# Macaron block on one core: uneven halves of the products with v, pieces behind the smaller half, row additions on GpSimd, VectorE's side work regrouped

## The chip, the core and the metric

One core of a Trainium2 chip runs the whole program. The metric is the device time of one execution in microseconds. TensorE (PE) multiplies, VectorE (DVE) and ScalarE (ACT) read the products from PSUM, GpSimd (POOL) works on SBUF alone, SyncE (SP) issues most DMAs. All data is float32.

## The reference, cut to what matters

```python
x = x + 0.5 * ffn(layernorm(x), ...)      # 8 experts, capacity 1.25 N / E; an expert chosen too often is dropped whole
x = x + attn(layernorm(x), ...)           # 16 heads of 16, causal softmax over 1024 tokens, 8 sequences
x = x + 0.5 * ffn(layernorm(x), ...)
# in ffn: probs = softmax(x @ gate_w.T); top 2 experts; keep = counts <= cap
```

x has 8 x 1024 tokens of 256 numbers. With these inputs every expert is chosen more often than its capacity allows, so both feed-forward parts add nothing; the kernel counts the choices of both gates in any case, and computes the experts only in a branch that this run does not enter. What is timed is the attention with its two gates.

## The kernel before, in words

The work goes by sequence b (8) and by group g of four heads (4): a **unit** u = 4 b + g, 32 in all. For each unit `project` makes q and k in transposed form (`pq`, one bank for each half of the tokens), packs them (`packed`) and sends them by DMA into `qTs` and `kTs` (four buffers each). Two passes over the scores follow.

- `m_steps` (line 852) multiplies q with k (`sm`), and VectorE takes the row maxima: `tensor_reduce` into `first` for a block wholly below the diagonal, a masked add-and-maximum (the row CUSTOM_DVE, with its DVE_READ_ACCUMULATOR into `top`) for a block that ends on it. `settle` transposes the maxima and sends them into a row of `qTs`.
- `e_steps` (line 898) multiplies k with q again (`sc`); the row of maxima is subtracted by the product itself. ScalarE takes the exponential into `pT`, GpSimd masks the diagonal block (the row TENSOR_SCALAR_AFFINE_SELECT), and `values` (line 927) multiplies by v, with a column of ones that gives the softmax's sums, into `pav`.

The two passes are interlaced by hand: at each of 24 **steps** k of a unit TensorE gets the `sc` tiles of unit u and the `sm` tiles of unit u + 1 in turn (line 1240), two of each, for one block and two heads. The widths of the blocks by step are 512, 512, 384, 384, 256, 256, 128, 128 for k = 0 to 7, then 512 eight times (k = 8 to 15, plain maxima), then again 512 down to 128 in pairs (k = 16 to 23, masked). Each step's tiles take four of six PSUM banks in rotation (`score`, line 700), so the third and fourth tile of a step take the banks of the first and second tile of the step before.

`values` of a block runs in two parts, at steps k + 2 and k + 3 (lines 1247 and 1248): the columns in two halves (line 937), or all in the first part when the block is 256 wide or less. So for the wide blocks part 0 falls on odd steps and part 1 on even ones.

Everything else goes **beside** the steps. A generator in `Beside` asks either for a number of steps to pass, or for a place: `PIECE` and `QK` wait until `step(kinds)` offers one, and `REST` asks for the next step, so that a matrix product of two halves is spread over two steps. After each step's products, `beside.step` is called once (lines 1278 to 1283): `QK` first at k = 0 and 8, `PIECE` at the steps in `long_steps` (0 to 3 and 8 to 19). Pieces are the four transposes of `turned`, the eight v products of `values_of` (`pv`) and the eight output products of `leave` (`px`) for each sequence. What a generator issues between its yields goes to the engines in the same place in their order:

- `prepare(b)` (732) loads x and takes its mean and variance on VectorE (`ln_stats`: BATCH_NORM_STATS2 and AGGREGATE) one tile of 128 rows every second step, from g = 3 on; `enter(b)` normalizes on GpSimd (`xn_a`) and transposes.
- `values_of` (774) copies v to `vaug` on ScalarE and the gate's logits on VectorE (799). `residual(b)` (805) adds the bias to x on GpSimd.
- `leave(b, hf)` (974) divides by the sums, multiplies with Wo into `px`, adds the row to x on VectorE (1017), and appends the statistics of the new row to `light`, one of which is taken at each step (1252). Then it stores the rows.
- `gate_first(b)` (815) and `regate(b)` (1103) choose two experts for each row (`choose`, 339: some twenty small VectorE operations named mx, lc, cand, first, oh, sm, prob, key, best, with an exponential on ScalarE; _f for the first gate and _g for the second) and add to a tally. `gate_first` starts at g = 0, k = 9; `regate` follows `leave(b - 1, 1)` and runs late in g = 1.

On every engine the order of issue is kept (`InOrder`, line 27), so an instruction that waits holds all behind it on its engine. Unit 31 has no scores of a next unit beside it and a loop of its own (line 1214), and `leave_last` finishes the last four heads.

Of the kernel before, what the change touches and what calls it, by code (L numbers as in the profile page):

```python
# [52 lines left out]
class Beside:  # L53
# [25 lines left out]

    def step(self, kinds=()):  # L80
        self.now += 1
        self.due()
        if self.open is not None:
            self.advance(self.open)
            return
        for kind in kinds:
            for work in self.works:
                if work[1] == kind:
                    self.advance(work)
                    return  # L90
# [12 lines left out]
def macaron_kernel(  # L103
# [112 lines left out]
    def weights(pool, bank, matmul, transpose):  # L216
# [15 lines left out]
        with nc.allow_non_contiguous_dma(reason="two vectors of 256"):  # L232
            nc.sync.dma_start(out=boT, in_=bo.rearrange("(c p) -> p c", p=P))
            nc.sync.dma_start(out=bvT, in_=bkv[D:].rearrange("(c p) -> p c", p=P))
        gpsimd.tensor_scalar(bkqT[64:], bkqT[64:], QSCALE, None, ALU.mult)

        def turn(wsb, dst, scale=None):
# [101 lines left out]
    def choose(rp, tag, n, lg):  # L339
        def new(name, shape=(P, n, E), dt=F32):  # L340
            return rp.tile(list(shape), dt, tag=f"{name}{n}", name=f"{name}_{tag}")

        def over_e(a):
            return a.unsqueeze(2).to_broadcast([P, n, E])

        mx = new("mx", (P, n))
        vector.tensor_reduce(mx, lg, AX.X, ALU.max)
        lc = new("lc")
        vector.tensor_tensor(lc, lg, over_e(mx), ALU.subtract)
        prob = new("prob")  # L350
        yield 1
        scalar.activation(prob, lc, AF.Exp)
        yield 1
        cand = new("cand")
        ohs = [new(f"oh{k}") for k in range(2)]

        def lowest(oh):
            vector.tensor_tensor(cand, cand, iota_e.unsqueeze(1).to_broadcast([P, n, E]), ALU.add)
            first = new("first", (P, n))
            vector.tensor_reduce(first, cand, AX.X, ALU.min)  # L360
            vector.tensor_tensor(oh, cand, over_e(first), ALU.is_equal)


        vector.tensor_scalar(cand, lc, 0.0, -100.0, ALU.is_equal, ALU.mult)
        lowest(ohs[0])
        yield 1
        sm = new("sm", (P, n))
        vector.tensor_reduce(sm, prob, AX.X, ALU.add)
        vector.reciprocal(sm, sm)
        vector.tensor_tensor(prob, prob, over_e(sm), ALU.mult)  # L370
        yield 1

        key = new("key")
        vector.tensor_scalar(key, prob, TINY, 1.0, ALU.is_ge, ALU.subtract)
        vector.scalar_tensor_tensor(key, key, 1e30, lc, ALU.mult, ALU.min)
        vector.scalar_tensor_tensor(key, ohs[0], -1e32, key, ALU.mult, ALU.add)
        yield 1
        best = new("best", (P, n))
        vector.tensor_reduce(best, key, AX.X, ALU.max)
        vector.tensor_tensor(cand, key, over_e(best), ALU.is_equal)  # L380
        yield 1
        vector.tensor_scalar(cand, cand, -100.0, None, ALU.mult)
        lowest(ohs[1])
        yield 1
        return prob, ohs
# [300 lines left out]
    def attention(run_no, src, dst, gate0, logits, tally):  # L686
# [3 lines left out]
        with stack:  # L690
# [40 lines left out]

            def prepare(b):
                xb = xbs[b] = ap.tile([P, TB, D + E], F32, tag="xa", name=f"xa{b}", bufs=3)
                nc.sync.dma_start(out=xb[:, :, :D], in_=src[b].rearrange("(j p) d -> p j d", p=P))
                yield 2
                st, mv = ln_tiles(f"a{b}")
                for j in range(TB):
                    ln_stats(xb, j, st, mv)
                    yield 2
                stds[b] = norm.tile([P, TB], F32, tag="std", name=f"std{b}")  # L740
                lns[b] = mv, ln_rstd(mv, f"a{b}", stds[b])
                yield 2
# [31 lines left out]
            def values_of(b, apart, j0=0, j1=TB):  # L774
# [7 lines left out]
                for j in range(j0, j1):  # L782
# [15 lines left out]
                    )  # L798
                    vector.tensor_copy(lg[:, j, :], pv[:, D : D + E])
                    if apart and j + 1 < TB:  # L800
# [22 lines left out]
            def project(u, parts=(0, 512)):  # L823
                b, g = divmod(u, NG)
                xnT = xnTs[b]
                for s0 in parts:
# [17 lines left out]
                    for k in range(8):  # L844
                        r = 32 * (k % 4)
                        nc.sync.dma_start(  # L846
                            out=(kTs, qTs)[k // 4][u % 4][r : r + HD, s0 : s0 + 512],
                            in_=packed[HD * k : HD * (k + 1), :],
                        )
# [48 lines left out]
            def e_steps(u):  # L898
# [28 lines left out]
                def values(hf, jb, pTs, part):  # L927
# [4 lines left out]
                    if w <= 256:  # L932
                        cols = slice(0, w)
                        if part == 1:
                            return
                    else:
                        cols = slice(part * w // 2, (part + 1) * w // 2)
                    for pr in (1, 0):
# [24 lines left out]
                for hf in range(2):  # L963
                    for jb in range(4 * hf + 4):
                        pTs = {}
                        yield (lambda h, hf=hf, jb=jb, pTs=pTs: scores(hf, jb, 1, pTs, h)), None
                        yield (
                            (lambda h, hf=hf, jb=jb, pTs=pTs: scores(hf, jb, 0, pTs, h)),
                            (lambda part, hf=hf, jb=jb, pTs=pTs: values(hf, jb, pTs, part)),
                        )  # L970

            def leave(b, hf):
# [28 lines left out]
                for i in range(TB // 2):  # L1003
# [3 lines left out]
                    for c in range(DC):  # L1007
# [7 lines left out]
                        if c + 1 < DC:  # L1015
                            yield REST
                    vector.tensor_tensor(xb[:, j, :], px[:, : D + E], xb[:, j, :], ALU.add)
                    light.append(lambda j=j: ln_stats(xb, j, *gate_lns[b]))
                rows = slice(hf * 512, hf * 512 + 512)
# [83 lines left out]
            def regate(b, j0, j1):  # L1103
# [4 lines left out]
                rstd = ln_rstd(gate_lns[b][1][:, j0:j1, :], f"g{b}_{j0}")  # L1108
                yield 3
                lg = logits[:, b * TB + j0 : b * TB + j1, :]  # L1110
# [32 lines left out]
            vaugs = [fixed.tile([P, TB, NH * VW + 32 - VW], F32, name=f"vaug{run_no}_{k}") for k in range(2)]  # L1143
            for qT in qTs:
                gpsimd.memset(qT, 0.0)
            for vaug in vaugs:
                gpsimd.memset(vaug[:, :, : NH * VW].rearrange("p t (h r) -> p t h r", r=VW)[:, :, :, HD:], 1.0)
                gpsimd.memset(vaug[:, :, NH * VW :], 1.0)
            for kT in kTs[:2]:
# [8 lines left out]
            for j0 in (0, HT):  # L1158
                for j in range(j0, j0 + HT):
                    ln_stats(xb, j, st, mv)  # L1160
                part = slice(j0, j0 + HT)
                rstds.append(ln_rstd(mv[:, part, :], f"a0_{j0}", stds[0][:, part]))
            for hf in range(2):
                xns = []
# [10 lines left out]
            opening = beside.add(chain(some(turning, 2), project(1), values_of(0, 0, 0, HT)))  # L1175
            owed, light, last, ons = deque(), deque(), [], {}
            STEPS = 24

            long_steps = [*range(4), *range(8, 20)]
            for u in range(-1, NU):  # L1180
                b, g = divmod(u, NG)
                if u == 0:
                    beside.finish(opening)
                    preparing = beside.add(prepare(1))
                    opening = beside.add(values_of(0, 0, HT, TB), first=True)
                    projecting = beside.add(project(2))
                    beside.add(chain((PIECE,), turning, residual(0), gate_first(0)))
                if u >= 0 and g == 2 and b + 1 < B:
                    beside.finish(entering)
                    valuing = beside.add(values_of(b + 1, 0, 0, HT))  # L1190
                if u >= 0 and g == 3 and b + 1 < B:
                    beside.finish(valuing)
                    valuing = beside.add(chain(values_of(b + 1, 0, HT, TB), residual(b + 1)))
                if u > 0:
# [3 lines left out]
                if g == 3 and u >= 0:  # L1198
                    if b + 2 < B:
                        preparing = beside.add(prepare(b + 2))  # L1200
                if u > 0 and g == 0:
# [12 lines left out]
                for k in range(0, STEPS, 2) if u == NU - 1 else ():  # L1214
# [10 lines left out]
                    if k == 0:  # L1225
                        beside.add(divided(b, 1, 8, 12, ons[1][:, 1], (1, 3, 3, 3)))
                    if k == 0:
                        beside.add(settle(u, 1), first=True)
# [8 lines left out]
                for k in range(STEPS) if 0 <= u < NU - 1 else ():  # L1237
# [11 lines left out]
                    while owed and owed[0][0] <= now:  # L1249
                        _, then, part = owed.popleft()  # L1250
                        then(part)
                    if light:
                        light.popleft()()
# [4 lines left out]
                    if g == 3 and k == 9:  # L1258

                        beside.add(leave(b, 0))  # L1260
                    if g == 0 and b and k == 9:

                        beside.add(gate_first(b))
                    if g == 0 and b and k == 2:
                        beside.add(chain(leave(b - 1, 1), regate(b - 1, 0, TB)))
                    if g == 1 and k == 7 and b + 1 < B:
# [11 lines left out]
                    if u == 0:  # L1278
                        beside.step((PIECE, QK))
                    elif k in (0, 8):  # L1280
                        beside.step((QK, PIECE))
# [9 lines left out]
            for k, _ in enumerate(leave_last(B - 1, 1, last.pop(), (scalar.copy, vector.tensor_copy))):  # L1291
                for _ in range(3 if k < 2 else len(beside.works) * STEPS):
                    beside.step()
# [65 lines left out]
```

## Time and profile before

| what | before |
| --- | --- |
| median of 3 runs | 1375.16 us (1372.16 to 1376.97) |
| the profiled execution | 1375.38 us |
| its span, first to last instruction | 1373.6 us |
| granted TensorE clock, mean | 0.987 |
| start of the first and of the last of the 744 interlaced steps | 53.6 us, 1318.9 us |
| length of a unit with g = 0, 1, 2, 3 (units 12 to 15) | 41.2, 42.4, 39.8, 39.9 us |
| copy of v to vaug, 128x256, ScalarE | 373 ns x 64 |
| addition of a row, xa<-px,xa, 128x264, VectorE | 427 ns x 64 |
| copy of logits, 128x8, VectorE | 159 ns x 64 |
| statistics of a tile, VectorE | 421 and 182 ns x 64 for each of st_g, mv_g |
| addition of the bias, 128x528, GpSimd | 1308 ns x 32 |

A row of a group has the line, the engine, the operation, the tiles written and read, the shapes and the count, then busy time and mean duration, then the idle time before it and what ended it. All operations of the attention are recorded at line 37, since they pass through `InOrder`, so groups are told apart by tiles. In a timeline the columns are start, duration, engine, line, operation, tiles, shapes, count, and in brackets the idle time before. One float32 matmul of the program shows as two instructions.

### The profile page before, as it was taken

How to read it: one execution, taken by the hardware profiler on the slowest of the kernel's cores; microseconds unless marked ns; L12 is line 12 of the kernel's file. 1: busy time of each engine (PE TensorE's matmuls, PEld its weight loads, DVE VectorE, ACT ScalarE, POOL GpSimd, SP SyncE). 2: the span in 40 equal slices, each digit the busy share in tenths (PEclk: the TensorE clock that was granted, in tenths of full speed). 3: DMA queues.
4: the chain of work that ended last, by engine and by line, in shares of the span. 5: the costliest groups of instructions: out<-in, count | busy, mean ns of one | idle time of the engine just before them, and what ended most of it. 6: DMA issues, size and time to landing. Idle time of an engine off the chain costs nothing.

```text
span 1373.6 us, 51244 instructions
## 1 busy us (share of the span) xinstructions
PE 1336.6 (97%) x20664; PEld 445.5 (32%) x20664; DVE 1038.2 (76%) x3417; ACT 785.5 (57%) x1790; POOL 398.1 (29%) x720
## 2 busy tenths in 40 slices
PE   6999999999999999999999999999999999999994
PEld 2333333333333333333333333333333333333331
DVE  3877677887787877877788777788777787787854
ACT  3256665565655565556665656656665556555562
POOL 3034114341235213152141411424123521312321
PEclk9899999999999999999999999999999999999997
DMA  4011111121121211212021211212112111121101
GB/s 142 18 27 42 42 43 56 55 72 42 53 65 49 83 31 48 74 52 77 21 58 60 84 46 37 60 57 73 42 54 58 53 49 34 50 74 42 60 27 34
DMA packets 67024, 73.73 MB, mean 54 GB/s; under 512 B 24688, under 2 KB 42232, under 8 KB 66776
## 3 DMA queue, kind: packets, MB, share of 16 engines
q1 hardware_dynamic: 65688, 69.82, 17.4%
q8 instruction: 165, 2.70, 0.8%
q14 instruction: 83, 0.68, 0.2%
q10 hardware_dynamic: 1088, 0.53, 0.1%
HBM read 26.87 MB, written 26.20 MB: 39 GB/s over the span
## 4 chain that ended last, share of the span: by engine, by line
PE 95%; DVE 3%; DMA 1%; issue 1%; POOL 0%; ACT 0%; SPq 0%; ACTq 0%; POOLq 0%
PE sc L37 42%; PE pav L37 24%; PE sm L37 10%; PE pq L37 9%; PE pv L37 5%; PE px L37 4%; PE pta L37 1%; DVE sm L37 1%; DMA bkqT<-in_L_attn_bq_dram 0%; DVE cand_g L37 0%; SPq L846 0%; PE px_last L37 0%; DVE top L37 0%; DVE first_g L37 0%; DVE oh_g L37 0%
## 5 line engine op out<-in xcount | busy, mean ns | idle before, releaser
L37 ACT ACTIVATE pT<-sc 128x512 f32<-128x512 f32 (+3 forms) x1536 | 668.9, 488 | 518.1 <-PE sm L37 381.4
L37 PE MATMUL sm<-kT,qT 32*64 32x512 f32 (+3 forms) x6144 | 752.8, 510 | 4.2 <-DVE top L37 2.2
L37 PE MATMUL sc<-qT,kT 32*64 32x512 f32 (+3 forms) x6144 | 693.8, 507 | 0.0
L37 DVE TENSOR_REDUCE first<-sm 128x1 f32<-128x512 f32 x512 | 328.7, 685 | 123.3 <-PE sm L37 122.6
L37 POOL TENSOR_SCALAR_AFFINE_SELECT pT<-pT 128x256 f32<-128x256 f32 x512 | 207.6, 408 | 735.4 <-ACT pT L37 734.9
L37 PE MATMUL pav<-pT,vaug 128*32 128x256 f32 (+2 forms) x5120 | 381.8, 370 | 2.2 <-POOL pT L37 1.5
L37 DVE CUSTOM_DVE_ANT_0 sm<-sm,causal 128x256 f32<-128x256 f32 (+3 forms) x512 | 241.8, 514 | 90.8 <-PE sm L37 80.3
L37 DVE CUSTOM_DVE_ANT_0 sm<-sm,causal,first 128x256 f32<-128x256 f32 (+3 forms) x512 | 261.4, 556 | 54.3 <-PE sm L37 48.5
L37 PEld LDWEIGHTS sc<-qT,kT 32*64 32x64 f32 x6144 | 183.1, 130 | 345.9 <-ACT pT L37 266.8
L37 PEld LDWEIGHTS sm<-kT,qT 32*64 32x64 f32 x6144 | 210.8, 130 | 33.4 <-DVE top L37 21.5
L37 PEld LDWEIGHTS pav<-pT,vaug 128*32 128x32 f32 x5120 | 102.5, 108 | 362.3 <-issue 282.7
L37 DVE DVE_READ_ACCUMULATOR2_ANT top<- 128x1 f32 x1024 | 145.5, 142 | 0.0
L37 PE MATMUL pq<-xnT,wkqT 128*32 128x512 f32 x1024 | 136.5, 608 | 1.3 <-ACT xnT L37 1.3
L37 PE MATMUL pv<-wvT,xnT 128*32 128x264 f32 x1024 | 81.1, 391 | 0.0
L37 PE MATMUL px<-woT,on 128*32 128x264 f32 x960 | 76.3, 390 | 0.0
L37 POOL TENSOR_SCALAR xn_a<-xa,mv_a,rstd_a 128x256 f32<-128x256 f32 x56 | 67.5, 1221 | 0.0
L37 ACT ACTIVATE packed<-pq,bkqT 128x512 f32<-128x512 f32 x64 | 45.4, 710 | 11.7 <-PE pq L37 11.7
L37 POOL TENSOR_TENSOR xa<-xa,bo_all 128x528 f32<-128x528 f32 x32 | 41.8, 1308 | 14.3 <-issue 13.7
L37 POOL TENSOR_TENSOR on<-on,inv 128x512 f32<-128x512 f32 (+1 forms) x32 | 40.3, 1282 | 14.1 <-DMA inv<-inv_d 14.1
L37 PEld LDWEIGHTS pq<-xnT,wkqT 128*32 128x32 f32 x1024 | 25.9, 110 | 55.5 <-issue 52.0
L37 PEld LDWEIGHTS pv<-wvT,xnT 128*32 128x32 f32 x1024 | 29.6, 110 | 41.8 <-ACT att L37 18.9
L37 PEld LDWEIGHTS px<-woT,on 128*32 128x32 f32 x960 | 27.3, 109 | 37.3 <-ACT att L37 11.4
(122 smaller groups left out, 430.8 us busy)
## 6 DMA issues: line engine op xcount, KB each, us to landing
att_d<-att SPq DMA_DIRECT2D x62, 256.0 KB
kT<-packed SPq DMA_DIRECT2D x256, 32.0 KB
qT<-packed SPq DMA_DIRECT2D x256, 32.0 KB
out_dram<-xa SPq DMA_DIRECT2D x16, 512.0 KB
on<-att_d SPq DMA_DIRECT2D x30, 256.0 KB
inv<-inv_d SPq DMA_DIRECT2D x30, 256.0 KB
xa<-in_L_attn_x_dram SPq DMA_DIRECT2D x7, 1024.0 KB
xa<-in_L_attn_x_dram SPq DMA_DIRECT2D x2, 512.0 KB
```

The costliest lines, as they stand in the source:

```text
L37: i = call(*args, **kwargs)
```

## The change

1. `values` cuts a block of 512 columns at 160 instead of 256; part 0 has 160 columns, part 1 has 352. Blocks of 384 are still halved.
2. For g other than 1 (and not in the last two units), pieces are begun only at k = 2, 10, 13 and 17, and the second half of a piece is not taken at k = 14 and 18, so it lands at 3, 11, 15 and 19. For g = 1 the places stay as they were.
3. In `leave`, ScalarE copies the product's row to SBUF (`row`), and GpSimd adds it to x, in steps k = 8 to 16 or at the end of `leave`. The rows of `leave_first` and `leave_last` are still added by VectorE.
4. Statistics in `light` are taken only at k = 8 to 15 of g = 1 and 2. `prepare` waits 32 steps after its load and then takes one tile at each step, which puts it at k = 8 to 15 of g = 0. `regate` starts at g = 2, k = 9, `gate_first` at g = 3, k = 8 (for the last sequence at the start of unit 31), `residual` at g = 0, k = 9. `choose` and `regate` yield less.
5. The logits are copied by ScalarE.
6. At the start, the scaling of bkqT and most memsets come behind the first statistics on GpSimd, and four of the eight DMAs of each packed half of unit 0 go to ScalarE's queue. In the tail one pause is shorter.

```diff
-    def step(self, kinds=()):
+    def step(self, kinds=(), rest=True):
...
         if self.open is not None:
-            self.advance(self.open)
+            if rest:
+                self.advance(self.open)
             return
...
-        gpsimd.tensor_scalar(bkqT[64:], bkqT[64:], QSCALE, None, ALU.mult)
...
         scalar.activation(prob, lc, AF.Exp)
-        yield 1
...
-            def prepare(b):
+            def prepare(b, wait, apart):
...
-                yield 2
+                yield wait
...
-                    yield 2
+                    yield apart
...
-                    vector.tensor_copy(lg[:, j, :], pv[:, D : D + E])
+                    scalar.copy(lg[:, j, :], pv[:, D : D + E])
...
-                        nc.sync.dma_start(
+                        (nc.scalar if u == 0 and k < 4 else nc.sync).dma_start(
...
-                        cols = slice(part * w // 2, (part + 1) * w // 2)
+                        cut = 160 if w == 512 else w // 2
+                        cols = slice(cut, w) if part else slice(0, cut)
...
+            def add_row():
+                xb, j, row, stats = adds.popleft()
+                gpsimd.tensor_tensor(xb[:, j, :], row, xb[:, j, :], ALU.add)
+                light.append(lambda: ln_stats(xb, j, *stats))
...
-                    vector.tensor_tensor(xb[:, j, :], px[:, : D + E], xb[:, j, :], ALU.add)
-                    light.append(lambda j=j: ln_stats(xb, j, *gate_lns[b]))
+                    row = ap.tile([P, D + E], F32, tag="row", name=f"row{b}_{j}", bufs=4)
+                    scalar.copy(row, px[:, : D + E])
+                    adds.append((xb, j, row, gate_lns[b]))
+                yield 2
+                while adds:
+                    add_row()
...
-                yield 3
+                yield 1
...
-            for qT in qTs:
-                gpsimd.memset(qT, 0.0)
-            for vaug in vaugs:
-                gpsimd.memset(vaug[:, :, : NH * VW].rearrange("p t (h r) -> p t h r", r=VW)[:, :, :, HD:], 1.0)
-                gpsimd.memset(vaug[:, :, NH * VW :], 1.0)
+            gpsimd.memset(qTs[0], 0.0)
...
-                    preparing = beside.add(prepare(1))
+                    preparing = beside.add(prepare(1, 2, 2))
...
-                    beside.add(chain((PIECE,), turning, residual(0), gate_first(0)))
+                    beside.add(chain((PIECE,), turning, residual(0)))
...
-                    valuing = beside.add(chain(values_of(b + 1, 0, HT, TB), residual(b + 1)))
+                    valuing = beside.add(values_of(b + 1, 0, HT, TB))
...
-                        preparing = beside.add(prepare(b + 2))
+                        preparing = beside.add(prepare(b + 2, STEPS + 8, 1))
...
-                    if light:
+                    if adds and 8 <= k <= 16:
+                        add_row()
+                    if light and 8 <= k < 16 and g in (1, 2):
                         light.popleft()()
...
-                    if g == 0 and b and k == 9:
-
+                    if g == 3 and k == 8:
                         beside.add(gate_first(b))
                     if g == 0 and b and k == 2:
-                        beside.add(chain(leave(b - 1, 1), regate(b - 1, 0, TB)))
+                        beside.add(leave(b - 1, 1))
+                    if g == 0 and b and k == 9:
+                        beside.add(residual(b))
+                    if g == 2 and b and k == 9:
+                        beside.add(regate(b - 1, 0, TB))
...
+                    elif g != 1 and u < NU - 2 and k not in (0, 8):
+
+                        beside.step((PIECE,) if k in (2, 10, 13, 17) else (), k not in (14, 18))
...
-                for _ in range(3 if k < 2 else len(beside.works) * STEPS):
+                for _ in range((1, 3)[k] if k < 2 else len(beside.works) * STEPS):
```

More of the change, by code (lines that the diff above doesn't have):

```diff
@@ L1162, in attention @@
                 rstds.append(ln_rstd(mv[:, part, :], f"a0_{j0}", stds[0][:, part]))
+            if gate0 is not None:
+                gpsimd.tensor_scalar(bkqT[64:], bkqT[64:], QSCALE, None, ALU.mult)
+            for qT in qTs[1:]:
+                gpsimd.memset(qT, 0.0)
+            for vaug in vaugs:
+                gpsimd.memset(vaug[:, :, : NH * VW].rearrange("p t (h r) -> p t h r", r=VW)[:, :, :, HD:], 1.0)
+                gpsimd.memset(vaug[:, :, NH * VW :], 1.0)
             for hf in range(2):
@@ L1175, in attention @@
             opening = beside.add(chain(some(turning, 2), project(1), values_of(0, 0, 0, HT)))
-            owed, light, last, ons = deque(), deque(), [], {}
+            owed, adds, light, last, ons = deque(), deque(), deque(), [], {}
             STEPS = 24
@@ L1226, in attention @@
                         beside.add(divided(b, 1, 8, 12, ons[1][:, 1], (1, 3, 3, 3)))
+                        beside.add(gate_first(b))
                     if k == 0:
```

## The prediction

> **What bounds the kernel now.** I read the page first, then the groups with shapes kept apart, then TensorE's and VectorE's timelines side by side.
>
> ```profile
> PE 1336.6 (97%) x20664; PEld 445.5 (32%) x20664; DVE 1038.2 (76%) x3417; ACT 785.5 (57%) x1790; POOL 398.1 (29%) x720
> ...
> PE 95%; DVE 3%; DMA 1%; issue 1%; POOL 0%; ACT 0%; SPq 0%; ACTq 0%; POOLq 0%
> ```
>
> The busy row and the chain both say TensorE, and the change removes no matmul. If 97% meant work, nothing could be won. But a waiting matmul whose neighbour runs still counts as busy, so I measured steps. A step (four score tiles, then products with v, then perhaps a piece) begins with its first score matmul; 744 of them (units 0 to 30, k 0 to 23) can be cut out of the timeline. Here are steps k=16, 17 and the start of 18 of a unit with g=2.
>
> ```profile
> 658.04 0.65 PE L37 MATMUL sc<-qT,kT 32*64 32x512 f32 x2
> 658.08 0.65 PE L37 MATMUL sm<-kT,qT 32*64 32x512 f32 x2
> ...
> 659.08 0.64 PE L37 MATMUL pav<-pT,vaug 128*32 128x256 f32 x8
> 659.65 0.64 PE L37 MATMUL sc<-qT,kT 32*64 32x512 f32 x2
> 659.66 0.65 PE L37 MATMUL sm<-kT,qT 32*64 32x512 f32 x2
> 659.87 0.65 PE L37 MATMUL sc<-qT,kT 32*64 32x512 f32 x2
> 660.09 0.64 PE L37 MATMUL sm<-kT,qT 32*64 32x512 f32 x2
> ...
> 661.10 0.64 PE L37 MATMUL pav<-pT,vaug 128*32 128x256 f32 x8
> 661.66 0.54 PE L37 MATMUL sc<-qT,kT 32*64 32x384 f32 x2
> ```
>
> In step 16 the fourth tile starts 0.04 us after the first, and the products follow at 1.04. In step 17 it starts 0.44 late and the products follow at 1.45: 0.40 us lost, with no gap shown. VectorE says why:
>
> ```profile
> 659.22 0.76 DVE L37 CUSTOM_DVE_ANT_0 sm<-sm,causal,first 128x512 f32<-128x512 f32 x1 [0.46 <-PE sm L37]
> 659.90 0.14 DVE L37 DVE_READ_ACCUMULATOR2_ANT top<- 128x1 f32 x1
> 659.90 0.75 DVE L37 CUSTOM_DVE_ANT_0 sm<-sm,causal,first 128x512 f32<-128x512 f32 x1
> ```
>
> Six banks serve four tiles a step, so a step's second pair reuses the banks of the previous step's first pair. That bank is free 2.01 us after the step's start (reading starts at 1.18, takes 0.76, and the flag's trip). Step 16 lasted 1.61, so step 17 lost 0.40. **Stall = release minus length.** Releases from such pairs: 2.01 for masked 512 columns, 1.89 for plain 512 (1.63 + 0.26), 1.67 for 384, 1.32 for 256. Unstalled score blocks take 1.044, 0.831, 0.617 and 0.404 us for 512, 384, 256 and 128 columns; the excess over these, summed over 744 steps, is 76 us, 5.5% of the span. It is the pool that this change can win from. By unit: 3.05 (g=0), 2.07 (g=1), 1.74 (g=2), 1.88 (g=3).
>
> The excess of g=0 is work of VectorE that stands ahead of the score tiles:
>
> ```profile
> 575.18 0.18 DVE L37 TENSOR_SCALAR cand_f<-cand_f 128x64 f32<-128x64 f32 x1
> ...
> 576.06 0.42 DVE L37 TENSOR_TENSOR xa<-px,xa 128x264 f32<-128x264 f32 x1
> 576.40 0.75 DVE L37 CUSTOM_DVE_ANT_0 sm<-sm,causal,first 128x512 f32<-128x512 f32 x1
> ```
>
> The score tile was readable at 575.83 (ScalarE starts on its neighbour then) and VectorE came at 576.40.
>
> **The change, part by part.** Step lengths first. Products of 128, 192 and 256 columns before scores take 0.355 (0.242 + the 0.113 below), 0.462 and 0.569 us: 0.142 + 1.67 ns a column. With a half piece behind, 0.113 less, and the half piece (264 columns) 0.559. So for 512-column scores:
> - before: alone 1.044 + 0.569 = 1.61; with a half piece 1.044 + 0.456 + 0.559 = 2.06.
> - after: 160 columns and a half piece 1.90; 352 columns alone 1.77; the pair 3.67 as before.
>
> TensorE's own work is unchanged: as many matmuls and columns. Only stalls can move.
>
> *Split and placement (g=0, 2, 3).* Half pieces go behind steps 2, 3, 10, 11, 13, 15, 17, 19 instead of 2, 3 and 10 to 15. By the rule, with no extra VectorE work: step 3 keeps 0.19, steps 5 and 6 together 0.25, step 11 keeps 0.26 (step 10 is 1.63 in both), 13 and 15 now lose 1.89 - 1.77 = 0.12 each, 17 loses 2.01 - 1.77 = 0.24 (was 0.40), 19 loses 1.67 - 1.56 = 0.11 (was 0.26), 22 keeps 0.24, 20 or 21 lose nothing (were 0.13 to 0.27). Sum 1.53. So smoothing alone is worth 0.2 to 0.35 us a unit: what 17 to 21 win, 13 and 15 partly give back.
>
> *VectorE's work.* It loses 56 row additions of 0.43 (24 us) and 64 copies of logits of 0.16 (10 us). Of the rest, statistics and routing choices now stand in steps 8 to 16 of different units. Room there: steps 10 to 16 last 1.63 + 3 x 1.90 + 3 x 1.77 = 12.6, plus stalls 0.5 = 13.1; VectorE's tiles take 6 x 1.20 + 1.34 = 8.6 (spacing 0.60 plain, 0.67 masked). The extra work put there, from the order of the instructions and the durations above (statistics 0.60 a tile row, choice operations 0.22, reciprocal 0.54):
> - g=0: eight statistics, of which 3.0 in steps 10 to 14 plus 0.6 and 0.54: 4.1; total 12.7, fits. Step 10 alone holds 1.14 and pushes step 12: up to +0.25. Today g=0 holds 8.3 in steps 9 to 16.
> - g=1: statistics only, pieces behind every step, no routing in the narrow steps 18 to 23 (today 21 to 23 lose 1.36): left are 0.19 + 0.25 + 0.26 + 0.24 + 0.1 = 1.0.
> - g=2: routing, 4.9; total 13.5, 0.4 too much: up to 1.9.
> - g=3: routing of the other gate, 3.7; 12.3, fits, early part pushes one step: up to 1.75.
>
> Applied to today's g=0 the same counting gives about 3.7 and the trace has 3.05, so I take half of the pushes: g=0 1.6, g=1 1.0, g=2 1.7, g=3 1.6. Against today: -1.45, -1.07, -0.04, -0.28, together -2.84 a batch, and seven batches make **-19.9**.
>
> *Additions on GpSimd.* The Trainium skill (GPSIMD Engine Reference, Engine selection) gives elementwise additions to VectorE, GpSimd being about twice as slow with two inputs. The row agrees on size: 528 columns take 1308 ns, so 264 about 0.65 (estimate) against 0.43, and ScalarE must first copy the row out (0.38, by the 256-column copy to vaug, 373 ns). Were engine time what counts, 56 x (0.65 + 0.38 - 0.43) = +34 us, 1409. By the waits view GpSimd idles 735 us for ScalarE's exponentials, and the adds stand where there is nothing to mask (k=8 to 16) or at k=21: I take 0. Behind an add wait the mask selects (0.41) and behind those the products two steps later: of a select that could start 2.27 us into step 17, the products come some 4.5 us into it, 1.8 us of cover after the 0.41. Behind the add on SyncE is the store of out and then the next qT rows, first needed eight steps later. If the cover is gone, each late select costs its lateness. Statistics follow their add by a step or more; only the last of g=1 shares one, and its add (row ready 0.55 into the step, 0.65) ends before VectorE gets there (2.47).
>
> *ScalarE* gains copies (0.38 x 56, about 0.2 x 64 for logits, 34 us) in the first 0.75 us of a step, before its exponentials at 1.18: 0; between 0 and +3 us, since exp's release (1.80) is just above 1.77.
>
> *Start.* rstd no longer waits for bkqT (rstd at 9.82, its input ready 7.6, but VectorE is busy to 10.06): -0.8. Four of eight kT/qT issues (0.6 each) go to ScalarE's queue; they delay one xnT copy there by some 2.4 us but free qT 2.5 earlier: together -1.1, between 0 and -2.5. *Unit 1* loses the routing work: -0.7, units 0 and 2: -0.3. *Unit 30*, with few pieces, takes regate's 4.9 us beside seven row additions: +1.4. *Last unit:* the first gate's last choice lies in VectorE's idle time, but the second half of att_last now stands behind eight choice operations: +0.6.
>
> Sum: -19.9 - 1.1 - 1.0 + 1.4 + 0.6 = -20.0. The profiled execution took 1375.38 (span 1373.6, 1.8 around it), 0.2 above the median of the runs, so 1355.4; I say 1355.5.
>
> **Rivals.**
> - *Little from the regrouping.* The pushes count in full and ScalarE's release binds after the 352s: g=0 1.85, g=2 2.0, g=3 1.9, and +3: -2.0 x 7 + 3 - 0.1 = -11, 1364. For it: total room and load in steps 10 to 16 are within 3%. Against: the rule overstates pushes today. 0.22.
> - *More than counted.* VectorE so relieved that 13, 15 and 17 hardly stall: a further -1.0 a batch, 1347. 0.11.
> - *Nothing.* The win of steps 17 to 21 reappears at 12 to 15 in each unit, g=1 alone gains, and unit 30, tail and start cost a little: within 4 us of 1375. 0.06.
> - *Slower: VectorE overruns its room.* Everything extra now stands in steps 8 to 16. The Trainium skill (SBUF — State Buffer, Who interferes with whom) has VectorE instructions with two SBUF inputs, or in a two-port mode, block against a reading GpSimd. A row looks like it: cand_g, run among mask selects, takes 357 ns where cand_f takes 209. At 1.6 times the routing's 8.6 us in g=2 and g=3 become 13.8 and none of the 5.2 more finds room: -2.5 + 5.2 a batch, 1394. It decides from 55 ns more on each of some 45 operations. Against it: g=2 and g=3 have no GpSimd work in steps 10 to 16 after the change, and g=0 and g=1 hold statistics, which read one tensor (421 and 417 ns, with and without company). 0.06.
>
> **How the numbers follow.** Forecast 0.55 (1350 to 1361), the rivals as given. The range 1346 to 1368 takes in the unknown bounds and most of both neighbours. Faster by over 0.3% (below 1371, about what a measurement can tell) 0.89, within 0.3% 0.05, slower 0.06.
>
> **What would show it.** Right: TensorE's matmul counts unchanged; step k=17 of g=0 loses about 0.25 where it lost 0.93, 18 loses nothing; 21 to 23 of g=1 together about 0.25; a new 0.12 at 13 and 15; g=2 and g=3 units within 0.3 of today's lengths, g=0 and g=1 shorter by 1.1 to 1.5; xa additions on GpSimd about 0.65. Wrong: product matmuls waiting for GpSimd, score matmuls waiting for ScalarE where they waited for VectorE, or g=2 longer by over 0.5.

## The result, and the profile after

The changed kernel takes 1353.27 us (median of 4 runs, 1352.01 to 1355.31) where the kernel before, on the same chip, takes 1375.7: ratio 0.9842, 95% interval 0.9819 to 0.9866. The profiled execution took 1352.37, with a span of 1350.6, 23.0 less than before, at a granted clock of 0.986 (0.987 before).

The busy row and the shares of the chain of waits, both from the page of the changed kernel:

```profile
PE 1316.8 (98%) x20664; PEld 438.2 (32%) x20664; DVE 1014.6 (75%) x3297; ACT 808.0 (60%) x1910; POOL 440.2 (33%) x776
PE 95%; DVE 2%; ACT 1%; issue 1%; POOL 1%; DMA 0%; ACTq 0%; POOLq 0%; DVEq 0%
```

TensorE has exactly as many matmuls as before and is busy 19.8 us less. Work was not removed; busy time that was waiting was. The chain has hardly moved, so neither line says where. Steps do. TensorE's timeline for the unit shown in the prediction (g = 2, steps k = 16, 17 and the start of 18, columns as there):

```profile
646.62 0.64 PE L37 MATMUL sc<-qT,kT 32*64 32x512 f32 x2
646.66 0.64 PE L37 MATMUL sm<-kT,qT 32*64 32x512 f32 x2
...
647.66 0.80 PE L37 MATMUL pav<-pT,vaug 128*32 128x352 f32 x8
648.39 0.65 PE L37 MATMUL sc<-qT,kT 32*64 32x512 f32 x2
648.40 0.65 PE L37 MATMUL sm<-kT,qT 32*64 32x512 f32 x2
648.45 0.64 PE L37 MATMUL sc<-qT,kT 32*64 32x512 f32 x2
648.73 0.65 PE L37 MATMUL sm<-kT,qT 32*64 32x512 f32 x2
...
649.74 0.48 PE L37 MATMUL pav<-pT,vaug 128*32 128x160 f32 x8
650.03 0.63 PE L37 MATMUL pv<-wvT,xnT 128*32 128x264 f32 x8
650.59 0.54 PE L37 MATMUL sc<-qT,kT 32*64 32x384 f32 x2
```

Step 16 is now 1.77 us long (it was 1.61); in step 17 the fourth tile starts 0.34 late instead of 0.44 and the products follow at 1.35 instead of 1.45. So 0.30 is lost where 0.40 was. The rule without extra work gives 0.24; two operations of VectorE on the tally stand ahead of the tiles there. VectorE's timeline at k = 16 and 17 of a unit with g = 0 has nothing left that keeps the score tiles waiting:

```profile
566.60 0.18 DVE L37 BATCH_NORM_AGGREGATE mv_a<-st_a 128x2 f32<-128x6 f32 x1
566.96 0.76 DVE L37 CUSTOM_DVE_ANT_0 sm<-sm,causal,first 128x512 f32<-128x512 f32 x1 [0.17 <-PE sm L37]
...
568.73 0.76 DVE L37 CUSTOM_DVE_ANT_0 sm<-sm,causal,first 128x512 f32<-128x512 f32 x1 [0.28 <-PE sc L37]
```

The steps start at 565.77 and 567.55, so the tiles are taken 1.19 and 1.18 into their step, the moment they can be read; before, the one of step 17 waited 0.57. Cut by steps in the way of the prediction, the stalls of all 744 steps fall from 76.2 to 54.2 us (median over units 4 to 27, by g = 0, 1, 2, 3):

| kernel | 0 | 1 | 2 | 3 | sum of stalls, us |
| --- | --- | --- | --- | --- | --- |
| before | 3.05 | 2.07 | 1.74 | 1.88 | 76.2 |
| changed | 1.57 | 0.88 | 1.65 | 1.51 | 54.2 |

### The profile page after: what moved, and what is told of

It is laid out like the page before. It is cut to its first block, busy times and chain, and to the rows that moved or that the text cites. A ratio compares the mean times of both kernels' runs of the same rounds, so it can differ in the third digit from the quotient of the medians.

```text
span 1350.6 us, 51515 instructions
## 1 busy us (share of the span) xinstructions
PE 1316.8 (98%) x20664; PEld 438.2 (32%) x20664; DVE 1014.6 (75%) x3297; ACT 808.0 (60%) x1910; POOL 440.2 (33%) x776
## 4 chain that ended last, share of the span: by engine, by line
PE 95%; DVE 2%; ACT 1%; issue 1%; POOL 1%; DMA 0%; ACTq 0%; POOLq 0%; DVEq 0%
PE sc L37 42%; PE pav L37 24%; PE pq L37 9%; PE sm L37 8%; PE pv L37 5%; PE px L37 4%; PE pta L37 1%; DVE first L37 1%; ACT kT L37 0%; PE px_last L37 0%; DVE st_g L37 0%; ACTq L845 0%; DVE xa L37 0%; POOL rstd_g L37 0%; DMA att_d<-att 0%
## 5 line engine op out<-in xcount | busy, mean ns | idle before, releaser
L37 PE MATMUL sm<-kT,qT 32*64 32x512 f32 (+3 forms) x6144 | 730.9, 508 | 0.0
L37 PE MATMUL pav<-pT,vaug 128*32 128x160 f32 (+4 forms) x5120 | 382.1, 370 | 2.8 <-POOL pT L37 2.0
L37 PEld LDWEIGHTS sm<-kT,qT 32*64 32x64 f32 x6144 | 205.5, 130 | 17.5 <-DVE top L37 5.9
L37 PE MATMUL px<-woT,on 128*32 128x264 f32 x960 | 76.2, 389 | 0.1
L37 POOL TENSOR_TENSOR xa<-row,xa 128x264 f32<-128x264 f32 x56 | 41.7, 745 | 50.1 <-ACT row L37 50.1
```

What stands on the lines that cost most here:

```text
L37: i = call(*args, **kwargs)
```

## The experiments

A row compares with the kernel before, run beside it on the same chip; the changed kernel stands at 0.9842. Where the text gives a difference between the times of two kernels in us, it is the difference of two ratios times the 1376 us of the kernel before, since the rows were not all measured on one chip. The last column is the sum of stalls in the score blocks, in us; a wait of the products is not in it.

| kernel | median, us | ratio, 95% | stalls |
| --- | --- | --- | --- |
| even parts | 1367.23 | 0.9929, 0.9913 to 0.9946 | 64.9 |
| old places | 1364.75 | 0.9912, 0.9896 to 0.9929 | 62.2 |
| both of these | 1355.51 | 0.9843, 0.9827 to 0.9860 | 56.3 |
| parts and places alone | 1371.95 | 0.9961, 0.9949 to 0.9974 | 71.9 |
| additions on VectorE | 1357.03 | 0.9858, 0.9842 to 0.9875 | 57.4 |
| GpSimd, two more | 1393.11 | 1.0130, 1.011 to 1.015 | 79.0 |
| GpSimd, one more | 1360.66 | 0.9896, 0.9881 to 0.9910 | 56.2 |
| choices at old places | 1397.80 | 1.0143, 1.0119 to 1.0167 | 97.3 |
| the same without the bias | 1387.50 | 1.0088, 1.0073 to 1.0103 | 87.1 |
| parts of 96 and 416 | 1358.43 | 0.9872, 0.9856 to 0.9889 | 59.1 |
| late last block, 224 of 384 | 1343.06 | 0.9766, 0.9751 to 0.9780 | 42 |

**Which half of the change wins.** Four kernels undo or isolate the parts (item 1 of the change) and the places (item 2). Even parts of 256 columns:

```diff
-                        cut = 160 if w == 512 else w // 2
+                        cut = w // 2
```

> The changed kernel (1353.3) with the products with v in even parts of 256 and 256 columns again; the new places of the half pieces and the work of the other engines stay. T (a step loses its release minus the length of the step before; the gain of the change comes mainly from VectorE's work in units with g=0 and g=1): the short steps that follow a product step alone are 1.61 instead of 1.77 us, so steps 13, 15, 17, 19 lose 0.28, 0.28, 0.40, 0.27 instead of 0.12, 0.12, 0.24, 0.11; about +0.47 us for each unit of g=0, 2, 3 and +0.06 for g=1, about +10 in all: 1363. R1 (the uneven parts and their places are what won): most of the 22 us is given back, 1370 or more.

The old places of the half pieces:

```diff
-                    elif g != 1 and u < NU - 2 and k not in (0, 8):
+                    elif False:
```

> The changed kernel with the half pieces at their old steps (2, 3, 10 to 15), the 160 and 352 columns kept. T: units of g=0, 2, 3 look like units that have no pieces moved: stalls of 0.19, 0.18, 0.26, then 0.24, 0.32, 0.43 in steps 17, 18, 20 and 0.24 in 22, about 1.87 us a unit, but nothing lost at 13 and 15: +0.9 a batch, +6 in all, 1359. R1: without the places the uneven parts are worth nothing, 1368 or more.

Both of these edits together:

> The changed kernel with even parts of 256 columns and the half pieces at their old steps: only GpSimd's additions and the regrouped work of VectorE are left of the change. T: units of g=0, 2, 3 lose 1.55 to 1.88 us each (1.57, 1.65, 1.51 in the changed kernel), g=1 as in the changed kernel: 1353 to 1359, say 1356. R1: 1370 or more.

The kernel before with items 1 and 2 alone:

> The kernel before (1375.5) with the parts of 160 and 352 columns and the new places of the half pieces alone; nothing moved between the engines and VectorE's work as it was. T: what 17 to 21 win, 13 and 15 give back, and VectorE's load in g=0 (its 16 us of extra work) still pushes score tiles: between -2 and +9, 1373 to 1384. R1 (parts and places are what won): about 1360.

Together the two edits cost nothing that the runs can tell (0.9843 against 0.9842; by the stalls some 2 us): the rest of the change, items 3 to 6, makes nearly the whole gain. R1 falls. Items 5 and 6 were not run by themselves; the start, item 6, is 1.0 us shorter. But either edit alone costs some 10 us. With even parts a step alone is 1.61 us, and with the new places one comes before each of steps 13, 15, 17 and 19; TensorE's timeline of steps 14 and 15 (g = 2) in the kernel with even parts:

```profile
649.52 0.65 PE L37 MATMUL sc<-qT,kT 32*64 32x512 f32 x2
...
651.14 0.64 PE L37 MATMUL sc<-qT,kT 32*64 32x512 f32 x2
651.15 0.65 PE L37 MATMUL sm<-kT,qT 32*64 32x512 f32 x2
651.36 0.65 PE L37 MATMUL sc<-qT,kT 32*64 32x512 f32 x2
651.45 0.65 PE L37 MATMUL sm<-kT,qT 32*64 32x512 f32 x2
...
652.46 0.64 PE L37 MATMUL pav<-pT,vaug 128*32 128x256 f32 x8
```

The fourth tile starts 0.31 late and the products come at 1.32 instead of 1.04: 0.28, which is 1.89 - 1.61. Units of g = 0, 2, 3 then lose 2.10. With the old places the steps after 15 are single ones while 12 to 14 are longer than they need be: 17, 18 and 20 lose 0.24, 0.33 and 0.43 (0.41, 0.29, 0.43 for g = 2), the sizes that the theory named. In the kernel before, the two together gained 0.39% (0.26 to 0.51), 5 us: g = 0 does not fall (3.08 for 3.05), for which my expectation was right, and g = 3 falls by 0.42, g = 1 by 0.23; at the low end I had -2, so the size was missed.

**Whether the amount of VectorE's work counts, or its place.** First the additions back on VectorE:

```diff
-                    row = ap.tile([P, D + E], F32, tag="row", name=f"row{b}_{j}", bufs=4)
-                    scalar.copy(row, px[:, : D + E])
-                    adds.append((xb, j, row, gate_lns[b]))
+                    vector.tensor_tensor(xb[:, j, :], px[:, : D + E], xb[:, j, :], ALU.add)
+                    light.append(lambda j=j: ln_stats(xb, j, *gate_lns[b]))
```

> The changed kernel (1353.3) with the row additions on VectorE again (no copy by ScalarE, no addition by GpSimd): 56 additions of about 0.43 us, 24 us of VectorE's time, come back into the steps where they stood. T: VectorE has that room except in front of one or two score tiles of a unit: 0 to +4, about 1355. R2 (what counts is how many instructions VectorE has in all): about +10, 1363.

VectorE is busy 16.7 us more than in the changed kernel and the time grows by about 2, within intervals that overlap. The stalls grow by 3.2, nearly all in g = 0 (1.92 instead of 1.57: step 13 loses 0.28 that was not there), unit 30 and unit 0. R2 falls: most of the additions cost nothing on VectorE.

Then the two routing steps back at their old places:

```diff
-                    if g == 3 and k == 8:
+                    if g == 0 and b and k == 9:
                         beside.add(gate_first(b))
...
-                        beside.add(leave(b - 1, 1))
+                        beside.add(chain(leave(b - 1, 1), regate(b - 1, 0, TB)))
...
-                    if g == 2 and b and k == 9:
-                        beside.add(regate(b - 1, 0, TB))
```

> The changed kernel with the two routing steps at their old places in the batch (the first gate's choice chained behind the residual, at g=0 from k=9; the other gate's chained behind the last rows), parts, places and GpSimd's additions kept. T: the work then stands in g=0's masked steps and g=1's narrow ones: g=0 about +2.5, g=1 about +1.15 us, 3.6 a batch, 1378. R2: VectorE has as much work in all as in the changed kernel, so at most 1358.

With the same 3297 instructions on VectorE the kernel is 3.1% slower. How the work is spread counts, and R2 falls again. But the price is 41 us and I had 25: g = 0 loses 5.75, not 4.1, g = 1 2.96, not 2.0. It is slower even than the kernel before, in which the choices began at the same places, since the statistics of `prepare` now stand in g = 0 as well: VectorE's instructions other than those on score tiles take 10.7 us in steps 9 to 16 of unit 12, where they took 7.0 before and take 5.5 in the changed kernel. So the 41 us price this crowding, not the old places alone. One more cause stands in the timelines of GpSimd and of VectorE at k = 12 and 13 of a unit with g = 0:

```profile
575.42 2.57 POOL L37 TENSOR_TENSOR xa<-xa,bo_all 128x528 f32<-128x528 f32 x2
```

```profile
576.50 0.20 DVE L37 RECIPROCAL sm_f<-sm_f 128x8 f32<-128x8 f32 x1
576.74 1.34 DVE L37 TENSOR_TENSOR prob_f<-prob_f,sm_f 128x64 f32<-128x64 f32 x1
578.00 1.28 DVE L37 TENSOR_REDUCE first<-sm 128x1 f32<-128x512 f32 x2
```

A product of 128x64 numbers takes 1.34 us, and 0.225 on average in the changed kernel. It ends 0.08 us behind GpSimd's second addition, and the maxima of step 13 (which starts at 577.00) wait behind it. The trace has seven such products, and each ends 0.08 to 0.10 us behind an addition; the eighth, in unit 0, runs beside none and takes 0.23. To see whether that is cause or coincidence, the additions of the bias were taken out:

```diff
-                    gpsimd.tensor_tensor(part, part, bo_all.unsqueeze(1).to_broadcast([P, 2, D + E]), ALU.add)
```

> The kernel with the routing steps at their old places (1397.8) without GpSimd's four additions of the bias to x for each sequence (so the bias is left out of the output). T3: in that kernel a VectorE product of two inputs, prob_f<-prob_f,sm_f, took 1.34 us instead of 0.23 while GpSimd ran such an addition (1.31), in each unit with g=0, and held the score tiles behind it; without them it takes 0.23 and g=0 units lose about 1.1 us less, 8 in all: about 1390 or less. R3 (the coincidence costs nothing, VectorE's amount of work does it): within 2 of 1397.8.

VectorE's timeline at the same place:

```profile
571.41 0.20 DVE L37 RECIPROCAL sm_f<-sm_f 128x8 f32<-128x8 f32 x1
571.65 0.23 DVE L37 TENSOR_TENSOR prob_f<-prob_f,sm_f 128x64 f32<-128x64 f32 x1
571.79 1.28 DVE L37 TENSOR_REDUCE first<-sm 128x1 f32<-128x512 f32 x2
```

0.23 again; step 13 loses 0.57 instead of 1.69, g = 0 units 1.11 less and nothing else in a batch changes, and the ratio falls from 1.0143 to 1.0088, 8 us. T3 holds: the addition is the cause. What makes the product wait for it, no run here shows; it fits the Trainium skill (SBUF — State Buffer, Who interferes with whom), by which a VectorE instruction with two SBUF inputs contends with a GpSimd instruction that reads SBUF, since its second input comes through a read port that the two share under an exclusive lock. The remaining 34 us are pushes of score tiles: in steps 12 to 17 of g = 0, where 9.6 us of other work still stand in steps 9 to 16 of unit 12, and in the narrow steps 20 to 23 of g = 1.

**Whether GpSimd's additions are hidden.** Two more instructions on each row, and in a second kernel one:

```diff
+                for _ in range(2):
+                    gpsimd.tensor_scalar(row, row, 1.0, None, ALU.mult)
                 gpsimd.tensor_tensor(xb[:, j, :], row, xb[:, j, :], ALU.add)
```

> The changed kernel with two more GpSimd instructions on each row ahead of its addition (each multiplies the row by 1.0, so the output stays what it was): the additions end later by more than their own time. T: GpSimd's additions are hidden, so nothing: 1353, within 2. Rival (the additions already reach the mask selects and through these the products): each of 49 additions later by 0.6 or more makes products late, 1360 or more.

My theory falls here: 40 us more than the changed kernel. Two rows of TensorE's waits in that kernel (columns: who waits for whom, us in total, times, longest); in the changed kernel the first is not among the rows, and the second has 2.0 us in 2 times:

```profile
PE sm L37 <- DVE first L37: 12.0, 6, 2.0
PE pav L37 <- POOL pT L37: 9.6, 8, 1.3
```

Two places, then. g = 1 units lose 3.1 to 4.0 in step 16: the statistics of a row wait for its addition, and the maxima stand behind them on VectorE. VectorE's timeline in step 16 of unit 9, which starts at 453.35 and loses 3.97:

```profile
455.19 0.43 DVE L37 BATCH_NORM_STATS2 st_g<-xa 128x6 f32<-128x256 f32 x1 [3.23 <-POOL xa L37]
455.65 0.18 DVE L37 BATCH_NORM_AGGREGATE mv_g<-st_g 128x2 f32<-128x6 f32 x1
455.75 1.25 DVE L37 TENSOR_REDUCE first<-sm 128x1 f32<-128x512 f32 x2
```

And g = 0 units are 1.73 longer with no stall in the score blocks: products wait for a mask select. GpSimd's timeline from k = 17 of g = 0 shows what I had overlooked; first in the changed kernel, then with one more instruction:

```profile
568.49 0.74 POOL L37 TENSOR_TENSOR xa<-row,xa 128x264 f32<-128x264 f32 x1
569.20 0.24 POOL L37 TENSOR_SCALAR ve_a<-mv_a 128x8 f32<-128x8 f32 x1
569.53 1.67 POOL L37 TENSOR_TENSOR rstd_a<-ve_a,half 128x8 f32<-128x8 f32 x1
571.28 0.20 POOL L37 TENSOR_TENSOR std<-ve_a,rstd_a 128x8 f32<-128x8 f32 x1
571.44 0.77 POOL L37 TENSOR_SCALAR_AFFINE_SELECT pT<-pT 128x256 f32<-128x256 f32 x2
```

```profile
570.63 0.87 POOL L37 TENSOR_SCALAR row<-row 128x264 f32<-128x264 f32 x1
571.59 0.75 POOL L37 TENSOR_TENSOR xa<-row,xa 128x264 f32<-128x264 f32 x1
...
572.75 1.67 POOL L37 TENSOR_TENSOR rstd_a<-ve_a,half 128x8 f32<-128x8 f32 x1
...
574.65 1.13 POOL L37 TENSOR_SCALAR_AFFINE_SELECT pT<-pT 128x256 f32<-128x256 f32 x3
```

Behind the addition stand three instructions that make rstd_a, 2.24 us from the first one's start to the select; only then come the selects of step 17, which the products of step 19 need.

> The changed kernel with one more GpSimd instruction on each row ahead of its addition (0.87 us each; the output stays what it was). The trace with two more showed two places: in g=0 the mask selects of step 19 stand behind the addition of step 17 and 2.1 us of GpSimd's work on rstd_a, and in g=1 the last row's statistics, with score tiles behind them, wait for the addition. T2 (cover at the first place used up already, a margin of about one such instruction left at the second): g=0 units longer by about 0.87, g=1 by 0 to 0.6: +6 to +10, 1360 to 1363. R2 (GpSimd is simply overloaded, so half of the 40 us that two instructions cost): g=0 and g=1 both by half of what they lost, 1373.

T2 holds, at 0.78 for 0.87. One more instruction delays the addition by 0.96 (570.63 to 571.59) and lengthens each g = 0 unit by 0.78; two delay it by 1.90 and lengthen it by 1.73. So the changed kernel has 0.17 to 0.18 us of cover there. In g = 1 one more costs 0.19, two cost over 3.

**Whether the part of 160 is sharp.** Parts of 96 and 416 columns:

```diff
-                        cut = 160 if w == 512 else w // 2
+                        cut = 96 if w == 512 else w // 2
```

> The changed kernel with parts of 96 and 416 columns. T: the steps alone grow from 1.77 to 1.87 us and those with a half piece shrink from 1.90 to 1.80, so 13, 15, 17, 19 lose less and the steps after a half piece begin to lose 0 to 0.2: about -0.1 a unit, -1.5 in all (-3 to 0): the best part is flat. R1 (the part is what wins): a change of more than 4 either way.

The expectation missed: 0.9872 is 0.3% above 0.9842, with intervals that overlap, where I had a gain. The stalls are 4.9 higher: g = 3 and g = 2 are flat (1.50 and 1.66 for 1.51 and 1.65, where I had -0.1), g = 0 gains a bigger push at 12 (0.34 for 0.23), g = 1, with pieces behind every step from 10 to 15, loses 0.28 after its short parts, and units 29 to 30 and 0 lose 2.2. A step with a half piece is 1.90 long at 160, just above plain tiles' 1.89, and 1.80 at 96.

**A version by the rule.** If stall is release minus length, the stalls left at steps 11, 3 and 22 come from steps 10 (1.63), 2 (1.41) and 21 (1.08), of which the first two are short because the products of the last block of 128 columns stand in the step before, beside half a piece of `project`:

```diff
-                        owed.append((now + 2, then, 0))
+                        owed.append((now + (3 if k in (7, 23) else 2), then, 0))
...
-                        cut = 160 if w == 512 else w // 2
+                        cut = 160 if w == 512 else 224
...
-                att_d = att_ds.pop((b, hf))
                 waits = (2, 6, 5, 9) if hf else (2, 4, 4, 5)
                 yield waits[0]
+                att_d = att_ds.pop((b, hf))
```

> The changed kernel with two numbers changed: the products of the last block of each half (128 columns) one step later (steps 10 and 2 instead of 9 and 1), and blocks of 384 columns cut at 224 instead of 192. T (stall = release minus length): step 10 grows from 1.63 to 1.85 us, so step 11 loses 0.05 instead of 0.26; step 2 grows from 1.41 to 1.63, so step 3 loses 0.04 instead of 0.19; step 21 grows from 1.08 to 1.13, so step 22 loses 0.19 instead of 0.24, step 6 about 0.13 instead of 0.18: -0.4 to -0.46 a unit, 29 units, -12 to -13: 1341. Rival (the copy of the products' bank by ScalarE now comes next to the piece's bank, and the piece or the next products wait for a bank): step 10 or 11 gets longer by 0.3 or more, 1353 or slower.

TensorE's timeline at steps 10 and 11 (g = 2):

```profile
629.00 0.65 PE L37 MATMUL sc<-qT,kT 32*64 32x512 f32 x2
...
630.04 0.43 PE L37 MATMUL pav<-pT,vaug 128*32 128x128 f32 x8
630.28 0.63 PE L37 MATMUL pv<-wvT,xnT 128*32 128x264 f32 x8
630.84 0.65 PE L37 MATMUL sc<-qT,kT 32*64 32x512 f32 x2
...
631.93 0.48 PE L37 MATMUL pav<-pT,vaug 128*32 128x160 f32 x8
```

Step 10 is 1.84 long and the products of step 11 follow at 1.09 instead of 1.30. The stalls come out as computed: step 11 loses 0.04 (0.17 for g = 3, where operations of the first gate's choice stand ahead of the tiles), step 3 nothing, 22 0.19, 6 0.13; units lose 1.06, 0.37, 1.14 and 1.13. 1343.06 us is 0.8% below the changed kernel by the ratios, whose intervals are apart. The rule that explained the trace also sized an edit ahead of its run: -12 to -13 us expected, -10.5 measured by the ratios, and the span is 11.4 shorter (1339.2 for 1350.6).

## Why the prediction was right, and where its sizes were off

The forecast was 1355.5 and the time 1353.3. Term by term, from the lengths of the units in the two traces:

| term | predicted, us | measured |
| --- | --- | --- |
| seven batches (units 3 to 29) | -19.9 | -22.9 |
| units 0 to 2 | -1.0 | +0.2 |
| unit 30 | +1.4 | +0.9 |
| start, to the first step | -1.1 | -1.0 |
| last unit and tail | +0.6 | -0.2 |

- **What bounds it.** Right, and the experiments rest on it: stall is release minus length. It gave the single steps of the changed kernel where no other work of VectorE stands ahead of the tiles (0.24 at 17, nothing at 18, 0.11 at 13 of g = 3 and at 15 of g = 0 and 2, 0.24 for 21 to 23 of g = 1) and most of those of four further kernels: even parts, old places, parts and places alone, the version by the rule. With routing ahead of the tiles, 13 and 17 of g = 2 lose 0.25 and 0.30.
- **VectorE's room.** Right in its mechanism. "Half of the pushes" was too much for g = 3 (1.51 for 1.6), where only step 15 is pushed, by 0.09. For g = 1 no push was counted; it loses 0.88 for 1.0, since steps 5 and 6 together lose 0.18 and not 0.25, in every unit, and the last 0.1 did not come. In g = 0 the push at step 12 came in full, 0.23 of the 0.25, and relieved step 13, so 1.57 for 1.6. g = 3 ends 0.36 shorter than before, outside the 0.3 that I gave. Taking half was a fit to one unit: the 8.3 us that were counted for today's g = 0 in steps 9 to 16 are 7.0 in unit 12 when its trace is cut into steps.
- **Split and placement.** "Smoothing alone is worth 0.2 to 0.35 us a unit" was too much. The sum of 1.53 was set against units of the kernel before, 1.74 and 1.88, that VectorE's work had already pushed. Unit 2, in which VectorE pushes no score tile, loses 1.54 before, 1.55 in the kernel with both edits and 1.45 in the changed one, so smoothing alone is worth 0.10: most of what 17 and 19 win, 13 and 15 give back, and 22 loses 0.24 where 21 and 22 lost 0.13 and 0.11. On the regrouped kernel it is worth 0.04 to 0.09 for a unit of g = 0, 2, 3 by the stalls and nothing that the times can tell (0.9843 and 0.9842); on the kernel before, 5 us, none of it in g = 0. That the forecast for the batches came out near is luck in part: it took the relief of VectorE and the smoothing together as one difference, so that most of what was put down to smoothing in g = 2 and 3 came from VectorE.
- **Additions on GpSimd: 0.** Right for the changed kernel, for a reason that fell. They take 745 ns, not 650, and at 0.9858 without them against 0.9842 the time cannot tell a gain from nothing. But the "1.8 us of cover after the 0.41" left out the rstd_a chain between an addition and the selects: the cover is 0.18. Had an addition taken more than 0.92 (an estimate: 0.745 + 0.18), each g = 0 unit would have begun to lose.
- **ScalarE.** Its copies take 381 and 173 ns (estimates 380 and 200) and TensorE's score tiles show no new wait for it.
- **Unit 1 and the last unit.** Half of the relief of unit 1 came (-0.35), and unit 0 is 0.6 longer, which I had as a small gain. The choices ahead of att_last cost nothing that the tail shows.
- **The rival of VectorE overrunning.** What it feared exists, 1.34 us for 0.23, but it stays away here because gate_first and regate stand in g = 3 and g = 2, where GpSimd has no large addition: prob_f and prob_g of 128x64 take 225 ns each, and cand_g, the row that raised the fear, fell from 357 ns to 184. Putting gate_first back into g = 0 brought it.

What stays open: how much of the remaining 34 us of the kernel with the old choices comes from the statistics beside them in g = 0, and how much from the fewer yields in `choose`; and what items 4 and 5 are worth each, since neither was run without the other.

## What to carry to other kernels

When the busiest engine shows 97%, cut its timeline into the steps of the schedule, and compare each step's length with the time until its oldest buffer is free again; the difference is the loss, step by step, and an edit that evens out lengths can be priced before it is run. Small work on another engine costs by what is queued behind it and by how much of it stands in the same few steps, more than by its sum over the kernel. Before calling a moved instruction hidden, list everything between it and the next instruction that someone waits for: here three small instructions left 0.18 us of a cover that had been put at 1.8.

## What the runs showed of the hardware

- A VectorE product of 128x64 with two SBUF inputs took 1.34 us beside GpSimd's 128x528 addition and 0.23 without it. The statistics of st_g, with one input, took a mean of 420 ns without and 418 with GpSimd work beside them (changed kernel, 25 and 31 of them).
- VectorE's operations with a number (TENSOR_SCALAR) on cand_f and cand_g, 128x64 with one tensor read, took a mean of 318 ns beside GpSimd work (15 of them) and 185 without (14), in the kernel before.
- GpSimd's two-input addition of 128x264 took 745 ns, its product with a number 0.87 us (kernel with two more); VectorE's addition of the same row, from PSUM, 428 ns.
- GpSimd's instruction that makes rstd_a, 128x8, takes 1.67 us, more than twice a row addition of 264 columns.
